# Two layers of a network, image by image: layer 0 of the next image worked off in pieces between the steps of layer 1

## The chip, the cores and the metric

The kernel runs on one core of a Trainium2 chip. A core has a matrix engine (PE, with its weight loads listed apart as PEld), a vector engine (DVE), a scalar engine (ACT), a general engine (POOL), queues that start transfers (SP's is the one used here for images), an on-chip memory SBUF of 128 partitions, and a small accumulator memory PSUM in eight banks that PE writes. Every engine takes its instructions in a fixed order, and instructions of different engines wait for each other through semaphores. The metric is the device time of one execution in microseconds; lower is better.

## The reference

The input x is [8, 256, 64, 64] in float32: 8 images, 256 channels, 64×64 pixels. Each layer normalises x in 32 channel groups (mean and variance per image and group) and adds its result to x. What matters of the code, cut:

```python
# layer 0 (x is the normalised input)
x1, x2, x3 = conv1x1(x, w1), conv1x1(x, w2), conv1x1(x, w3)      # 32, 32, 256 channels
h = relu(bn(concat([x1, unfold3x3(reflect_pad(x2))])))            # 320 channels
h = relu(bn(conv1x1(h, cw1)))                                     # 32 channels
w = conv1x1(h, cw2)                                               # 32 groups x 9 taps per pixel
out0 = sum over 9 taps of unfold3x3(zero_pad(x3)) * w             # 8 channels share a group's weights
x = x + out0
# layer 1 (x normalised again)
q, k, v = conv1x1(x, Wq) / 8, conv1x1(x, Wk), conv1x1(x, Wv)      # 4 heads of 64
att = softmax(q . (unfold7x7(k) + position))                      # 49 neighbours of a pixel
out_att = att @ unfold7x7(v)
wts = softmax over 9 of conv1x1(x, Wfc)                           # 9 weights per channel and pixel
oc = dwconv3x3(relu(dwconv3x3(x, w1)), w2)
out1 = rate1 * out_att + rate2 * sum over 9 of oc * wts
x = x + out1
```

## The kernel before

Channels lie on partitions, in two halves (ct = 0, 1); an image is cut into 8 bands of 8 rows, so that a tile [128, 512] is one half of one band. The images run strictly one after the other: all of layer 0, then all of layer 1, each with pools of its own. A band of x stays in SBUF from its load to its store (`xpool`, 10 band tiles): layer 0 writes its result over it, and layer 1 adds to it. The zero-padded map x3 (`x3p`) and the normalised padded image (`yp`, 70×70) are whole images and share one buffer. The order of instructions on each engine is made when the program is built, by a scheduler that follows program order and free buffers; a buffer with n copies lets n users be in flight.

Layer 0, with L numbers of the profile: `small_maps` (one matmul pair p12 and six ACT writes into x2s), `value_maps` (p3, L260, then an ACT write into x3p), `hidden_maps` (three relu writes, three matmuls ph at L283, h2), `products` (three pw matmuls at L295 into one tile of three banks, one DVE multiply of 128×1536 at L300, one POOL add of 128×1536 at L305), and `add_up` (an ACT copy of x into PSUM at L312, three DVE adds at L313 to L315, then bn_stats at L168 for the normalisation of layer 1). The loop staggers them by hand: maps of band i, hidden of band i − 1, products of band i − 2.

Layer 1 starts with `gn_affine` (normalisation constants), writes yp with ACT (L352) and the reflected pads with POOL. Then per band: `values` (pv matmuls at L418, ACT copies, transposes pvt at L432, ACT copies vt at L434), `place` (position term, POOL, L443), and for each ct `queries_keys` (pq L459, pk L475, DVE adds kb at L479, a POOL copy at L470), `depthwise` (ACT starts acc at L548 and L566, DVE taps at L560 and L573, ACT copy oc at L578) and four m-steps. An m-step is `probabilities` (mask and scores sco at L496 and L500, nmax on DVE at L505, exponentials and scaling on ACT at L510 and L515, the reciprocal tot on DVE at L513), the `weighted_values` of the step before (transposes ptp L522, ACT copy pt L524, 16 po matmuls L529) and `branch_weights` (two pf results of two matmuls each at L588, ACT exponentials ex at L593, and from the second step a DVE add of 128×1024 at L595). After the fourth step `dynamic_sum` closes the half: L603 adds the two halves of the sum on DVE, L604 bounds it, L606 takes the reciprocal `rec`, POOL multiplies twice (L608, L610), and DVE adds the result to x (L611); L390 adds po. Then the band is stored and band i of the next image is loaded into the freed tile, with its bn_stats.

PSUM in layer 0 is two `gen` banks and two pw tiles of three banks; in layer 1 three `gen` banks (pv, pvt, pq, pk, pf), two for sco, one each for po, acc and ptp.

## Time and profile before

| what | value |
|---|---|
| median of 3 runs (lowest to highest) | 5641.66 us (5640.54 to 5642.27) |
| profiled execution, its own time | 5641.8 us |
| its span (first to last instruction) | 5639.2 us |
| mean granted PE clock | 0.965 |
| busy: PE, DVE, ACT, POOL | 5083.2, 4177.2, 3052.5, 1392.0 us |
| DMA traffic | 76.36 MB, mean 14 GB/s |
| landing of one x load, one store | 3.7 us, 2.7 us |

The profile is one execution. Its groups give for each line of the kernel the busy time, the mean length of one instruction in ns, and what the engine waited for before it. The windows give the busy time of every engine in a stretch of the span. The chain of waits follows the work that ended last back to what released it. A busy PE is not PE at its peak, since the ends of matmuls are modelled.

### The profile page before, as it was taken

Reading aid. Unit: us, or ns where it says so; the run is one execution under the profiler, and the core shown is the slowest. Engines: PE = TensorE matmul, PEld = TensorE weight load, DVE = VectorE, ACT = ScalarE, POOL = GpSimd, SP = SyncE. Lnnn points to the kernel's source line nnn. Section 1 sums busy time; section 2 is a strip of 40 time slices with the busy share of each in tenths; the row PEclk is TensorE's granted clock in tenths of the full one; section 3 lists DMA queues with packets and bytes.
Section 4 is the critical chain, followed back from the end, with each engine's and each line's share of the span. In section 5 each row is a group of like instructions: output and inputs, shape, how many; then the busy total and the mean of one; then the engine's idle time right before and its main releaser. Section 6 shows DMA issues by size and latency. Waiting matters only on the chain.

```text
span 5639.2 us, 71792 instructions
## 1 busy us (share of the span) xinstructions
PE 5083.2 (90%) x28064; PEld 2489.7 (44%) x28064; DVE 4177.2 (74%) x5709; ACT 3052.5 (54%) x7026; POOL 1392.0 (25%) x889
## 2 busy tenths in 40 slices
PE   6799987999879998799987999879998799997998
PEld 2345433454334543354433544335543354433544
DVE  5688756887568875688766887668866688666886
ACT  3466644665436654466544665446664466544665
POOL 3411044111441114411144111531115311153111
PEclk9899998999989999899998999989999899998999
DMA  1000000000000000000000000000000000000000
GB/s 71 1 16 20 20 8 0 16 23 16 8 0 16 23 16 8 1 16 23 16 8 1 16 23 16 8 1 23 16 16 8 1 23 16 12 4 1 12 8 12
DMA packets 37922, 76.36 MB, mean 14 GB/s; under 512 B 2768, under 2 KB 4432, under 8 KB 37328
## 3 DMA queue, kind: packets, MB, share of 16 engines
q1 hardware_dynamic: 34816, 67.12, 3.6%
q8 instruction: 221, 3.62, 0.3%
q10 hardware_dynamic: 2768, 4.66, 0.2%
q14 instruction: 117, 0.96, 0.1%
HBM read 38.22 MB, written 33.55 MB: 13 GB/s over the span
## 4 chain that ended last, share of the span: by engine, by line
PE 46%; DVE 30%; ACT 11%; POOL 9%; issue 4%; DMA 1%; POOLq 0%; ACTq 0%; DVEq 0%; SPq 0%
PE pf L588 19%; PE pw L295 7%; DVE rec L606 7%; DVE acc L573 4%; PE po L529 4%; POOL prod L305 4%; DVE prod L300 4%; PE p L260 4%; PE ptp L522 3%; DVE acc L560 3%; PE ph L283 3%; POOL ex L608 3%; POOL oc L610 3%; ACT ex L593 2%; PE sco L500 2%
## 5 line engine op out<-in xcount | busy, mean ns | idle before, releaser
L588 PE MATMUL pf<-yp,c_wfc 128*128 128x512 f32 x4096 | 2026.8, 614 | 0.0
L305 POOL TENSOR_TENSOR prod<-prod,prod 128x1536 f32<-128x1536 f32 x256 | 880.8, 3441 | 536.1 <-DVE prod L300 530.5
L300 DVE TENSOR_TENSOR prod<-pw,x3p 128x1536 f32<-128x1536 f32 x384 | 665.3, 1752 | 387.0 <-PE pw L295 381.7
L588 PEld LDWEIGHTS pf<-yp,c_wfc 128*128 128x128 f32 x4096 | 692.5, 188 | 566.7 <-issue 528.8
L593 ACT ACTIVATE ex<-pf 128x512 f32<-128x512 f32 x1024 | 609.4, 597 | 581.4 <-PE pf L588 574.3
L560 DVE SCALAR_TENSOR_TENSOR acc<-yp,c_chan,acc 128x504 f32<-128x504 f32 (+3 forms) x1104 | 773.0, 700 | 184.7 <-ACT acc L548 165.9
L573 DVE SCALAR_TENSOR_TENSOR acc<-hid,c_chan,acc 128x504 f32<-128x504 f32 (+3 forms) x1024 | 755.1, 737 | 91.2 <-ACT acc L566 74.8
L295 PE MATMUL pw<-h,c_c 64*128 64x512 f32 x2304 | 711.7, 652 | 82.9 <-DVE prod L300 82.6
L595 DVE TENSOR_TENSOR ex<-ex,ex 128x1024 f32<-128x1024 f32 x384 | 469.8, 1223 | 245.6 <-ACT ex L593 243.7
L608 POOL TENSOR_TENSOR ex<-ex,rec 128x512 f32<-128x512 f32 x128 | 162.5, 1270 | 1971.4 <-DVE rec L606 1769.4
L510 ACT ACTIVATE prob<-sco,nmax 128x196 f32<-128x196 f32 x1024 | 425.3, 422 | 245.5 <-DVE nmax L505 243.9
L295 PEld LDWEIGHTS pw<-h,c_c 64*128 64x128 f32 x2304 | 278.3, 197 | 501.1 <-issue 315.1
L515 ACT ACTIVATE prob<-prob,tot 128x196 f32<-128x196 f32 x1024 | 412.7, 454 | 88.0 <-DVE tot L513 81.3
L529 PEld LDWEIGHTS po<-pt,vt 112*64 112x64 f32 (+1 forms) x8192 | 281.7, 137 | 366.8 <-ACT pt L524 330.8
L524 ACT COPY pt<-ptp 112x512 f32<-112x512 f32 x512 | 299.6, 585 | 243.4 <-PE ptp L522 241.5
L606 DVE RECIPROCAL rec<-ex 128x512 f32<-128x512 f32 x128 | 427.9, 3343 | 0.3
L522 PE MATMUL ptp<-ident,prob 128*112 128x128 f32 x2048 | 337.0, 284 | 46.0 <-ACT prob L515 46.0
L529 PE MATMUL po<-pt,vt 112*64 112x64 f32 (+1 forms) x8192 | 353.5, 228 | 15.6 <-ACT pt L524 11.8
L418 PE MATMUL pv<-yp,c_wv 128*128 128x280 f32 (+1 forms) x1152 | 314.8, 420 | 57.9 <-POOL yp L366 47.2
L443 POOL TENSOR_TENSOR pe<-pecol,perow 128x560 f32<-128x560 f32 (+1 forms) x64 | 77.7, 1214 | 1128.9 <-DVE kb L479 1110.0
L505 DVE TENSOR_REDUCE nmax<-sco 128x2 f32<-128x392 f32 x512 | 284.0, 555 | 67.4 <-PE sco L500 66.1
L522 PEld LDWEIGHTS ptp<-ident,prob 128*112 128x112 f32 x2048 | 211.1, 133 | 230.0 <-ACT prob L515 120.4
(118 smaller groups left out, 5785.8 us busy)
## 6 DMA issues: line engine op xcount, KB each, us to landing
x<-in_x SPq DMA_DIRECT2D x64, 512.0 KB, 3.7
out_x<-x SPq DMA_DIRECT2D x64, 512.0 KB, 2.7
c_wfc<-in_wfc ACTq DMA_DIRECT2D x1, 2304.0 KB, 14.9
c_c<-in_c ACTq DMA_DIRECT2D x1, 640.0 KB, 8.1
c_w<-in_w ACTq DMA_DIRECT2D x1, 256.0 KB, 6.9
c_wq<-in_wq ACTq DMA_DIRECT2D x1, 256.0 KB, 7.9
c_wk<-in_wk ACTq DMA_DIRECT2D x1, 256.0 KB, 8.6
c_wv<-in_wv ACTq DMA_DIRECT2D x1, 256.0 KB, 9.9
```

What stands on the lines that cost most here:

```text
L295: nc.tensor.matmul(pw[:, dj], c2[s, k // NG, ct * P : (ct + 1) * P], h2[s, :], start=True, stop=True)
L300: nc.vector.tensor_mul(prod.rearrange("p k (r c) -> p k r c", r=R), pw, bass.AP(v.tensor, v.offset, [v.ap[0], (1, 3), v.ap[1], v.ap[2]]),)
L305: nc.gpsimd.tensor_add(sums[0], sums[0], prod)
L510: nc.scalar.activation(prob[:, h, :NKEY], sco[:, h, :NKEY], AF.Exp, bias=nmax[:, h : h + 1], accum_out=tot[:, h : h + 1])
L522: nc.tensor.transpose(ptp[:, h, ch], prob[:, h, ch * CHUNK : (ch + 1) * CHUNK], ident)
L529: nc.tensor.matmul(po[h * HD : (h + 1) * HD, :, (2 * m + t) * TQ : (2 * m + t + 1) * TQ], vts[ch][m][:n, t, (2 * ct + h) * HD : (2 * ct + ...
L560: nc.vector.scalar_tensor_tensor(o, yp[:, ct, ra + dr : rb + dr, ca + dc : cb + dc], chan[:, ct, CW1 + k : CW1 + k + 1], o, ALU.mult, ALU.add,
L573: nc.vector.scalar_tensor_tensor(o, hid[:, ra + dr : rb + dr, ca + dc : cb + dc], chan[:, ct, CW2 + k : CW2 + k + 1], o, ALU.mult, ALU.add,)
L588: nc.tensor.matmul(pf, wfc[:, kt, 2 * m + j, ct * P : (ct + 1) * P], yp[:, kt, i * R + PAD : i * R + PAD + R, PAD : PAD + W], start=(kt == ...
L593: nc.scalar.activation(ex[:, j].rearrange("p (r c) -> p r c", r=R), pf, AF.Exp)
L595: nc.vector.tensor_add(ex, ex, tot)
L606: nc.vector.reciprocal(rec, tot)
```

## The change

Layer 0 becomes a generator of small pieces, each with a weight: begin 1, small_maps 4, value_maps 4 per half, hidden_maps 6, products 3 for each of six groups, and zero for statistics and store: 36 per band, 289 per image. Layer 1 becomes a generator that yields twice in each m-step, 128 times per image. All layer 0 of image 0 and the pieces of 24 further steps (LEAD) are issued first; then each yield adds 289/128 to a credit, and pieces of the next images are issued as long as the credit covers them. So the pieces of layer 0 of image b + 1 stand in program order between the m-steps of layer 1 of image b.

Both layers now share all pools. All layer-0 results in PSUM (p12, p3, ph, pw) use the three gen banks of layer 1. Images no longer stay in SBUF: x is loaded twice (for its statistics, `x_s`, and for the work, `x_c`), the layer-0 result of each band is stored to a DRAM tile `x1`, and layer 1 reads it twice: as `xr` (the residual) and as `yp`, now a band tile of 14 rows with three buffers, filled by up to six transfers, then normalised in place on ACT and padded on POOL. All three kinds of x tile share five buffers. x2, x3 and vc become band tiles, and halo rows are copied by POOL.

Some operations move or change size. The multiply of 128×1536 becomes three of 128×512, the POOL add too; `add_up` becomes one POOL add to x (called xb in the text). The ex add of 128×1024, the add of the two halves and the last add to x go from DVE to POOL. The oc copy on ACT takes the scale rate2. ex has three buffers where it had four. The core of the diff:

```diff
+LEAD = 24
-    xpool = ctx.enter_context(tc.tile_pool(name="xpool", bufs=10))
-    img = ctx.enter_context(tc.tile_pool(name="img", bufs=1))
+    w0 = ctx.enter_context(tc.tile_pool(name="l0", bufs=2))
+    w1 = ctx.enter_context(tc.tile_pool(name="l1", bufs=2))
+    ps = ctx.enter_context(tc.tile_pool(name="ps", bufs=1, space=PSUM))
+    dram = ctx.enter_context(tc.tile_pool(name="dram", bufs=3 * NB, space=DRAM))
+    def x_tile(name):
+        return w0.tile([P, NCT, BAND], F32, tag="x", name=name, bufs=5)
...
+        def products(i, ct, di):
+            for dj in range(3):
+                k = 3 * di + dj
+                s = slice(k % NG * KG, (k % NG + 1) * KG)
+                pw = ps.tile([P, R, W], F32, tag="gen", name=f"pw_{b}_{i}_{ct}_{k}", bufs=3)
+                nc.tensor.matmul(pw, c2[s, k // NG, ct * P : (ct + 1) * P], h2s[i][s, :], start=True, stop=True)
+                prod = w0.tile([P, R, W], F32, tag="prod", name=f"prod_{b}_{i}_{ct}_{k}", bufs=5)
+                nc.vector.tensor_mul(prod, pw, x3s[i][:, ct, di : di + R, dj : dj + W])
+                if k == 0:
+                    sums[ct] = prod
+                else:
+                    nc.gpsimd.tensor_add(sums[ct], sums[ct], prod)
+            if di == 2:
+                xb = xs[i][:, ct, :]
+                nc.gpsimd.tensor_add(xb, xb, sums[ct].rearrange("p r c -> p (r c)"))
+                bn_stats(im.st1, xs[i], ct, i)
+        def store(i):
+            t = dram.tile([P, NCT, BAND], F32, tag="x1", name=f"x1_{b}_{i}")
+            im.x1.append(t)
+            nc.sync.dma_start(out=t, in_=xs[i])
+        yield 1, begin
+        for i in range(NB + 1):
+            if i < NB:
+                yield 4, lambda i=i: small_maps(i)
+                yield 4, lambda i=i: value_maps(i, 0)
+                yield 4, lambda i=i: value_maps(i, 1)
+            if b + 1 < B and i:
+                yield 0, lambda i=i: first_stats(b + 1, i - 1)
+            if i:
+                yield 6, lambda i=i: hidden_maps(i - 1)
+                for ct in range(NCT):
+                    for di in range(3):
+                        yield 3, lambda i=i, ct=ct, di=di: products(i - 1, ct, di)
+                yield 0, lambda i=i: store(i - 1)
+    def padded_band(b, i):
...
+        yp = w1.tile([P, NCT, RP, WP], F32, tag="yp", name=f"yp_{b}_{i}", bufs=3)
...
+        for ct in range(NCT):
+            nc.sync.dma_start(out=yp[:, ct, PAD : PAD + R, PAD : PAD + W], in_=x1[i][:, ct])
+            if i:
+                nc.sync.dma_start(out=yp[:, ct, :PAD, PAD : PAD + W], in_=x1[i - 1][:, ct, R - PAD :])
+            if i < NB - 1:
+                nc.sync.dma_start(out=yp[:, ct, PAD + R :, PAD : PAD + W], in_=x1[i + 1][:, ct, :PAD])
...
-        nc.scalar.copy(oc, acc)
+        nc.scalar.activation(oc, acc, AF.Copy, scale=rate2)
...
-        ex = w1.tile([P, 2, BAND], F32, tag="ex", name=f"ex_{nm}_{m}", bufs=4)
+        ex = w1.tile([P, 2, BAND], F32, tag="ex", name=f"ex_{nm}_{m}", bufs=3)
...
-            nc.vector.tensor_add(ex, ex, tot)
+            nc.gpsimd.tensor_add(ex, ex, tot)
...
-        nc.vector.tensor_add(tot, tot, even)
+        nc.gpsimd.tensor_add(tot, tot, even)
...
-        nc.vector.scalar_tensor_tensor(xs[i][:, ct], o, rate2, xs[i][:, ct], ALU.mult, ALU.add)
+        nc.gpsimd.tensor_add(xr[:, ct], xr[:, ct], o)
...
+    work = [list(layer0(b)) for b in range(B)]
+    steps = NB * NCT * NT
+    total = sum(w for w, f in work[1])
+    def advance(passes):
+        nonlocal credit
+        credit += passes
+        while queue and queue[0][0] <= credit:
+            w, f = queue.pop(0)
+            credit -= w
+            f()
+    advance(sum(w for w, f in work[0]) + total * LEAD / steps)
     for b in range(B):
+        for _ in layer1(b):
+            advance(total / steps)
```

In layer 1 the yp band i + 2 is prepared in the third m-step of band i's first half, and bands 0 and 1 of the next image in the last band's second half. The names, shapes and operations of the rest are unchanged.

## The prediction

> **What bounds the kernel now.** I read the busy row and the slices first, then the windows of the stages, then the chain of waits, then the groups.

> ```profile
> PE 5083.2 (90%) x28064; PEld 2489.7 (44%) x28064; DVE 4177.2 (74%) x5709; ACT 3052.5 (54%) x7026; POOL 1392.0 (25%) x889
> PE   6799987999879998799987999879998799997998
> POOL 3411044111441114411144111531115311153111
> 41.00:232.00 191.00, 160.01 (x441) 61.61 (x440) 127.14 (x123) 70.23 (x113) 112.34 (x35) 0.93 0.00 0
> 232.00:260.00 28.00, 20.12 (x81) 14.63 (x82) 10.22 (x20) 23.59 (x39) 4.55 (x18) 0.78 0.00 1
> 730.00:742.00 12.00, 4.28 (x17) 4.06 (x18) 5.30 (x17) 0.20 (x1) 2.52 (x2) 0.50 0.27 88
> 1864.00:1923.00 59.00, 58.32 (x378) 29.87 (x377) 51.35 (x75) 36.51 (x92) 7.21 (x7) 1.00 0.06 19
> ```

> The four windows give length, then busy time of PE, its weight loads, DVE, ACT and POOL, then the granted clock. They are layer 0 of image 0 (191 us), the start of its layer 1 (28), the gap before image 1 (12) and one steady layer-1 band (59.0). An image takes about 700 us. In a steady layer-1 band PE is busy 58.32 of 59.00 at clock 1.00: PE is the limit. Outside the steady bands PE loses: about 31 us in layer 0, 8 and 8 at the two seams. POOL works in layer 0 and almost rests in layer 1 (7.21 of 59).

> ```profile
> PE 46%; DVE 30%; ACT 11%; POOL 9%; issue 4%; DMA 1%; POOLq 0%; ACTq 0%; DVEq 0%; SPq 0%
> L305 POOL TENSOR_TENSOR prod<-prod,prod 128x1536 f32<-128x1536 f32 x256 | 880.8, 3441 | 536.1 <-DVE prod L300 530.5
> L300 DVE TENSOR_TENSOR prod<-pw,x3p 128x1536 f32<-128x1536 f32 x384 | 665.3, 1752 | 387.0 <-PE pw L295 381.7
> L595 DVE TENSOR_TENSOR ex<-ex,ex 128x1024 f32<-128x1024 f32 x384 | 469.8, 1223 | 245.6 <-ACT ex L593 243.7
> L608 POOL TENSOR_TENSOR ex<-ex,rec 128x512 f32<-128x512 f32 x128 | 162.5, 1270 | 1971.4 <-DVE rec L606 1769.4
> L606 DVE RECIPROCAL rec<-ex 128x512 f32<-128x512 f32 x128 | 427.9, 3343 | 0.3
> L603 DVE TENSOR_TENSOR ex<-ex 128x512 f32<-128x512 f32 x128 | 87.7, 685 | 0.8
> L479 DVE SCALAR_TENSOR_TENSOR kb<-pk,c_chan,pe 128x280 f32<-128x280 f32 (+1 forms) x288 | 138.3, 488 | 13.3 <-PE pk L475 13.3
> ```

> The chain of waits is PE for less than half and DVE for 30%: the queues hand over to each other closely. The groups give the prices: an add of 512 is 0.685 us on DVE (L603) and 1.270 on POOL (L608); one of 1536 is 3.441 on POOL. The add of 1024 on POOL has no row; between 1.270 and 3.441 a line gives 2.36 against DVE's 1.223 (L595).

> **What the change offers: the PE floor.** The matmuls stay. A layer-1 band cannot go under about 57.5 us of PE, a layer-0 band costs PE 18.8 when full; pw's nine 512-column matmuls per half alternate in pairs, and a stranger between them breaks the pairing, which I put at 2.5 us a band (between 0 and 4.5, by the 0.43 us that one record of a lone pw adds). Together 78.8 us for a joint band, against 59.2 + 19.8 = 79.0 now. So the floor gains nothing in the bands; what it removes is the lost PE time at the seams, 68 us per image (700 − 8 × 78.8). At this floor the program would take 5,370 us, worked out under the first rival.

> **What it moves to POOL.** Per image DVE loses L595 (48 × 1.223 = 58.7), L603 (16 × 0.685 = 11.0), L611 (12.9) and L313–315 (33.3), and gains about 15 by splitting 1752 ns products into three of 0.69: 522 to 421 us. ACT stays near 382 (the 512-wide copies into accumulators go, a wider yp normalisation comes; the two normalisations per image may cost up to two table loads of 1.28 each). POOL goes from 174 to about 419: product adds 128 × 1.27 = 162, ex adds 48 × 2.36 = 113, totals 20, multiplies 41, two residual adds 40, place, pads and halo copies 43. That is 54 us per joint band, below PE's 78.8. No engine's sum is the bound; the question is the waits.

> **Steady joint band, walked in queue order.** Every engine takes its queue in order, so an operation that waits holds those behind it.

> Step 1, between the channel halves. The last ex exp (0.60) now leads to POOL add 2.36, POOL add 1.27, then DVE tensor_scalar 0.42 and rec 3.34. Before, the kb adds (L479) of the next half stood ahead of rec; in the changed order they stand behind it. Starting from pq, kb ends at 0.8 + 2.4 + 1.3 + 0.4 + 3.4 + 2 × 0.49 ≈ 9.4 us. PE has pq, two pk pieces, ptp, po to do until 5.8, and its next matmul needs the bank that kb frees at 9.0: a stall of 3.2 us. Before, this cost nothing.

> Step 2, in the second half. bn_stats(st1) on DVE waits for POOL's xb add, which stands behind rec's two multiplies and the product adds (POOL lags by 13 us at that point, 1.27 per add). Behind bn_stats in DVE's queue stand the products whose reads free the three gen banks, so PE's pw and pf wait: 1.8 and 3.7 us. A stall already taken in step 1 lets POOL catch up, so I take half, 2.75 (range 0 to 5.5).

> Step 3, at the end of the band. rec → POOL multiply, multiply, xr add (3 × 1.27) → ACT oc copy, because oc has two buffers. In bands 1 to 3 of an image oc stands ahead of the next band's vt copies, acc and qb in ACT's queue, and vt frees the banks of pvt; in bands 4 to 7 it stands behind vt. From the last pf to the next band's first pf I count 21.9 us for 12.2 of PE work, a stall of 9.7, or 6.7 in the later bands: mean 7.8.

> Band: 78.8 + 3.2 + 2.75 + 7.8 = 92.6 us. All steps at full size give 95.3; step 3 alone gives 86.6; none gives 78.8.

> **Layer 0 of image 0, alone.** It has nothing beside it. Eighteen POOL adds of 1.27 (22.9) bound a band, plus about 6 us from halo copies through hid, ph, h2 to the first pw, since the pieces of one band now stand in program order without the two-band stagger: 29 us against 19.8. Start 41 + prologue 10 + (8 + 1.5 bands of lead) × 29 = 326 us until image 0's layer 1 begins (232 before).

> **The tail.** Layer-0 work ends 24 steps early, so image 7 and the end of image 6 (9.5 bands) run alone at about 64 us: 59.2 + 2.3 (kb behind rec) + 2.8 (oc behind POOL); 60 to 68.

> **Transfers.** x is read twice, the layer-0 result goes out and comes back twice, on SP's queue in order: x1 store (waits for xb), x_s, x_c, xr, six yp loads per band with rows of 256 B. These are 3,584 packets a band. A 2 KB packet of the x queue takes 3.6% × 16 × 5639 / 34816 = 0.093 us; at that price 3584 / 16 × 0.093 = 21 us, asked for more than a band ahead: hidden by the band, and I take zero (below zero is excluded, since all of it is added traffic; above, the third rival). [...]

> POOL's add keeps its length beside a busy DVE here: L305 runs from 3417 to 3462 ns over all 256. [...]

> **Sum.** 326 + 54.5 joint bands × 92.6 (5,047) + 7 images × 16.5 (values of band 0, 8.5; layer-1 normalisation and first yp, 8: 115) + 9.5 × 64 (608) + 9 (end, and 2.6 outside the span) = 6,105 us. The profiled run of before was 5641.8 (span 5639.2), as good as the median, 5641.66. Break-even is a joint band of (5641 − 326 − 115 − 608 − 9) / 54.5 = 84.1 us.

> **Rivals.**
> 1. PE-bound, faster: POOL's lag never reaches PE, as banks and buffers cover it. Band 79.5, tail 60: 326 + 4,333 + 115 + 570 + 9 ≈ 5,355. For it: no engine's sum passes PE, and POOL has 25 us of slack a band. Against it: three gen banks serve all of both layers, and kb and oc follow POOL chains of 4 to 8 us. It decides when the stalls sum to under 5.3 us a band; then the seams' 68 us win.
> 2. Only the end of the band stalls (step 3): 86.6, so 326 + 4,720 + 115 + 608 + 9 = 5,778, a slight loss. It decides if step 1's bank is freed in time and DVE never waits for xb.
> 3. DRAM traffic: 256-B rows at over 4.4 times 0.093 us make yp the wait; a band then takes 100 or more, 6,510. For it: the SP queue is one and in order; against: DMA is 1% busy.

> **Chances.** Forecast (bands of 88 to 100) 0.50; rival 2 with its neighbourhood (82 to 88) 0.20, of which a quarter lies under break-even; rival 1 0.24; rival 3 0.06. Faster 0.24 + 0.04 = 0.28; within 0.2% (about what this measurement can tell from nothing) 0.02; slower 0.70. The forecast's own range is 5,850 to 6,500; eight in ten needs rival 2 and the edge of rival 1: 5,420 to 6,500.

> **What would show it.** In the changed profile: joint bands of 88 to 97 us with PE busy 80 to 88% and POOL near 55 us; PE's idle put down to kb, to products on DVE, and to vt; DVE idle put down to POOL's xb and ex; 29 us per band before image 0's layer 1; bands of 64 at the end. Wrong if joint bands are under 84 us with PE above 95%, or if yp loads end the waits.

## The result, and the profile after

The changed kernel takes 6407.3 us (median of 4 runs, 6405.0 to 6408.6) against 5641.3 (4 runs): 1.136 times as long, 95% interval 1.134 to 1.138. The forecast was 6,105 us, slower, with a range of 5,420 to 6,500. The profiled run is 6405.0 us, its span 6403.2.

The busy row, the slices, the granted clock and the chain of the changed kernel:

```profile
PE 5583.4 (87%) x28064; PEld 2642.8 (41%) x28064; DVE 3437.2 (54%) x5453; ACT 3067.9 (48%) x6910; POOL 3282.2 (51%) x3049
...
PE   6788888888898888988898888988888988899988
...
PEclk8788999999999999999999999999999999999999
...
POOL 4744454554554545545455455544455454553443
...
PE 54%; POOL 21%; DVE 14%; ACT 5%; issue 4%; DMA 1%; POOLq 0%; SPq 0%; ACTq 0%; DVEq 0%
```

The work moved as the forecast had it: POOL 1392 to 3282 us (410 an image, 419 forecast), DVE 4177 to 3437 (430 an image, 421 forecast). No engine is the bound, and yet the span grew. PE's number of matmuls is the same, but its busy time rose by 500 us. About 340 of them are a lower clock: with PE's busy time laid on the profile's clock records, half speed cost 94 us in the kernel before and 434 here. What makes up the other 160 was not measured apart; the forecast had put 2.5 us in each of the 64 bands, 160 in all, on broken pairs of pw.

Windows of the changed kernel: layer 0 of image 0, one joint band (band 1 of image 2), one band of the tail. The columns are those of the windows before.

```profile
42.00:320.00 278.00, 227.29 (x460) 88.83 (x459) 120.38 (x196) 65.14 (x105) 189.94 (x194) 0.79 0.20 59
2055.30:2154.10 98.80, 85.91 (x433) 40.17 (x432) 52.36 (x80) 47.07 (x108) 51.22 (x47) 0.91 0.13 38
5930.00:5995.00 65.00, 57.85 (x362) 28.68 (x362) 46.28 (x71) 38.52 (x95) 27.27 (x23) 0.97 0.12 31
```

In the joint band PE is busy 85.9 of 98.8 us at a granted clock of 0.91: 85.9 × 0.91 = 78.2 us of full-speed work, close to the forecast's 78.8. The rest is idle (12.9) and slow clock (7.7). The product is an estimate, since the granted clock is a mean over the stretch with its idle time; the clock records laid on the busy time alone give 79.1 and 6.8. The idle is put down to these releasers, in the waits of PE over two joint bands:

```profile
PE pvt L456 <- ACT vt L458: 7.0, 2, 4.0
PE pf L611 <- DVE prod L313: 5.7, 2, 2.8
PE pw L311 <- DVE kb L502: 5.1, 2, 2.5
PE pvt L456 <- ACT vc L447: 3.8, 2, 2.4
PE pv L442 <- ACT ex L616: 2.8, 2, 1.4
PE pv L442 <- ACT x L251: 1.4, 2, 0.7
```

Halved, they are 2.5 us at kb (step 1), 2.8 at the products (step 2) and 7.5 at the end of the band, where step 3 lies. Of these 7.5, only 3.5 are the wait for vt that step 3 named; the other rows are vc, ex and the writes of x2s (L251). What each idle does to the clock is seen in PE's timeline (start, length, operation, idle before and its releaser) and in windows of 4 us around the first of them:

```profile
2193.60 0.69 PE L552 MATMUL po<-pt,vt 112*64 112x64 f32 x16
2196.83 1.12 PE L311 MATMUL pw<-h,c_c 64*128 64x512 f32 x2 [2.54 <-DVE kb L502]
...
2211.05 1.13 PE L311 MATMUL pw<-h,c_c 64*128 64x512 f32 x4
2215.00 3.62 PE L611 MATMUL pf<-yp,c_wfc 128*128 128x512 f32 x4 [2.83 <-DVE prod L313]
```

```profile
2190.00:2194.00 4.00, 4.00 (x30) 2.34 (x30) 1.33 (x2) 1.26 (x2) 2.52 (x2) 1.00 0.00 0
2194.00:2198.00 4.00, 1.46 (x16) 0.56 (x16) 3.80 (x5) 0.00 (x0) 1.40 (x2) 0.98 0.00 0
2198.00:2202.00 4.00, 4.00 (x12) 1.42 (x13) 1.77 (x3) 0.53 (x1) 4.00 (x4) 0.50 0.02 4
2202.00:2206.00 4.00, 4.00 (x7) 1.48 (x6) 3.73 (x7) 2.98 (x9) 3.64 (x4) 0.67 0.00 0
2206.00:2210.00 4.00, 4.00 (x25) 1.63 (x24) 3.39 (x7) 1.11 (x2) 1.59 (x2) 1.00 0.00 0
```

After 2.54 us of idle the clock is 0.50 for about four microseconds and 0.67 in the mean over the next four. This stall of 2.5 us thus cost about 6: 2.0 us are lost in the first four and 1.3 in the next. The forecast had no term for this in its bands.

The groups that answer to those of before, and two that show the new waits (the third number is the idle time of the engine ahead of the group):

```profile
L317 POOL TENSOR_TENSOR prod<-prod,prod 128x512 f32<-128x512 f32 x1024 | 1298.3, 1268 | 606.5 <-DVE prod L313 544.7
L618 POOL TENSOR_TENSOR ex<-ex,ex 128x1024 f32<-128x1024 f32 x384 | 903.4, 2353 | 1259.6 <-ACT ex L616 1259.6
L627 DVE TENSOR_SCALAR ex<-ex 128x512 f32<-128x512 f32 x128 | 75.8, 592 | 660.3 <-POOL ex L626 649.4
L177 DVE BATCH_NORM_STATS2 st<-x_c 128x6 f32<-128x512 f32 x128 | 88.9, 694 | 472.3 <-POOL x_c L320 472.3
L601 ACT ACTIVATE oc<-acc,c_rowp 128x512 f32<-128x512 f32 x128 | 88.0, 687 | 533.7 <-POOL xr L634 525.6
```

The POOL add of 1024 takes 2.353 us; the interpolation said 2.36. The last three rows are the three places where a queue stands still for POOL: ahead of rec (L627), at bn_stats (L177) and at the oc copy (L601). The experiments ask which of them costs PE time.

### The profile page after: what moved, and what is told of

It is laid out like the page before. It is cut to its first block, busy times and chain, and to the rows that moved or that the text cites. A ratio compares the mean times of both kernels' runs of the same rounds, so it can differ in the third digit from the quotient of the medians.

```text
span 6403.2 us, 75865 instructions
## 1 busy us (share of the span) xinstructions
PE 5583.4 (87%) x28064; PEld 2642.8 (41%) x28064; DVE 3437.2 (54%) x5453; ACT 3067.9 (48%) x6910; POOL 3282.2 (51%) x3049
## 3 DMA queue, kind: packets, MB, share of 16 engines
q1 hardware_dynamic: 293376, 223.39, 12.5%
## 4 chain that ended last, share of the span: by engine, by line
PE 54%; POOL 21%; DVE 14%; ACT 5%; issue 4%; DMA 1%; POOLq 0%; SPq 0%; ACTq 0%; DVEq 0%
PE pf L611 26%; PE pw L311 8%; POOL prod L317 8%; DVE rec L629 6%; POOL ex L618 4%; PE po L552 3%; PE sco L523 3%; PE ph L298 3%; PE p L276 3%; PE ptp L545 3%; POOL x_c L320 2%; POOL ex L626 2%; DVE prod L313 2%; PE pq L482 2%; DVE acc L583 2%
## 5 line engine op out<-in xcount | busy, mean ns | idle before, releaser
L611 PE MATMUL pf<-yp,c_wfc 128*128 128x512 f32 x4096 | 2157.0, 659 | 142.6 <-DVE prod L313 123.3
L317 POOL TENSOR_TENSOR prod<-prod,prod 128x512 f32<-128x512 f32 x1024 | 1298.3, 1268 | 606.5 <-DVE prod L313 544.7
L618 POOL TENSOR_TENSOR ex<-ex,ex 128x1024 f32<-128x1024 f32 x384 | 903.4, 2353 | 1259.6 <-ACT ex L616 1259.6
L611 PEld LDWEIGHTS pf<-yp,c_wfc 128*128 128x128 f32 x4096 | 779.8, 206 | 1113.0 <-issue 773.3
L311 PE MATMUL pw<-h,c_c 64*128 64x512 f32 x2304 | 957.6, 688 | 149.0 <-DVE kb L502 88.8
L313 DVE TENSOR_TENSOR prod<-pw,x 128x512 f32<-128x512 f32 x1152 | 752.2, 683 | 338.9 <-PE pw L311 317.0
L627 DVE TENSOR_SCALAR ex<-ex 128x512 f32<-128x512 f32 x128 | 75.8, 592 | 660.3 <-POOL ex L626 649.4
L601 ACT ACTIVATE oc<-acc,c_rowp 128x512 f32<-128x512 f32 x128 | 88.0, 687 | 533.7 <-POOL xr L634 525.6
```

Source lines behind the costliest of these rows:

```text
L311: nc.tensor.matmul(pw, c2[s, k // NG, ct * P : (ct + 1) * P], h2s[i][s, :], start=True, stop=True)
L313: nc.vector.tensor_mul(prod, pw, x3s[i][:, ct, di : di + R, dj : dj + W])
L317: nc.gpsimd.tensor_add(sums[ct], sums[ct], prod)
L611: nc.tensor.matmul(pf, wfc[:, kt, 2 * m + j, ct * P : (ct + 1) * P], yp[:, kt, PAD : PAD + R, PAD : PAD + W], start=(kt == 0), stop=(kt == ...
L618: nc.gpsimd.tensor_add(ex, ex, tot)
```

## The experiments

Theory T: the joint band is about 79 us of matmul work, 13 of idle behind chains that end on POOL, and the slow clock after it. Rival M: the mixing costs, because three gen banks serve two layers, whoever adds. The first four kernels:

**The three adds back on DVE.**

```diff
-            nc.gpsimd.tensor_add(ex, ex, tot)
+            nc.vector.tensor_add(ex, ex, tot)
...
-        nc.gpsimd.tensor_add(tot, tot, even)
+        nc.vector.tensor_add(tot, tot, even)
...
-        nc.gpsimd.tensor_add(xr[:, ct], xr[:, ct], o)
+        nc.vector.tensor_add(xr[:, ct], xr[:, ct], o)
```

> Edit: the ex add, the add of the two halves and the add to xr go back from POOL to DVE; all else as changed. Theory T (the joint band of 98.5 us is 79 us of matmul work, about 13 us of PE idle behind chains that pass through POOL, and about 6.5 us of matmul time at the lowered clock that follows these idles): the chain ahead of rec gets 1.7 us shorter (2.36 to 1.22, 1.27 to 0.69), the one behind it 0.6; the stall at kb falls from 2.7 to about 1 us and takes no clock any more, the end of the band loses 2 to 3 us of idle: band about 92, time about 6050. Rival M (the mixing itself: two layers through three gen banks stall PE whoever does the adds): DVE's 10 us more per band delay the products that free the banks: no gain, 6400 or more.

Measured: 6047 us, 360 less. Three joint bands take 269.6 us for 297.8 (image 3, bands 1 to 3). The bands of image 7, which have no layer 0 beside them, fall to 58.7 to 60.1 us (64.5 in the first, and not counting the last, which runs to the end of the kernel), where they had been 64.2 to 68.2: with the adds on DVE, layer 1 alone is back at the 59.2 of before. T holds, and M has no account of it.

**bn_stats later in program order.**

```diff
-                bn_stats(im.st1, xs[i], ct, i)
+                late.append((xs[i], ct, i))        # issued ahead of the next half's third product group
...
```

> Edit: bn_stats of a layer-0 half is issued one half later, so that DVE does not wait for POOL's last add to x; the add itself stays where it is. T: the stall of pf behind a product behind bn_stats (3.4 us in a joint band) goes, and with it the half clock that follows: 5 us a band, time about 6130. Rival M: the bank wait comes back at the next product, since the banks are short anyway: under 1 us a band, 6350 or more.

Measured: 6407 us, no change. That is M's number and not T's, but the timelines of DVE show that the edit did not do what it was meant to; of the changed kernel:

```profile
2209.95 0.56 DVE L528 TENSOR_REDUCE nmax<-sco 128x2 f32<-128x392 f32 x1
2213.66 0.69 DVE L177 BATCH_NORM_STATS2 st<-x_c 128x6 f32<-128x512 f32 x1 [3.16 <-POOL x_c L320]
2214.28 0.67 DVE L313 TENSOR_TENSOR prod<-pw,x 128x512 f32<-128x512 f32 x1
```

and of this one:

```profile
2211.17 0.56 DVE L537 TENSOR_REDUCE nmax<-sco 128x2 f32<-128x392 f32 x1
2214.89 0.69 DVE L177 BATCH_NORM_STATS2 st<-x_c 128x6 f32<-128x512 f32 x1 [3.16 <-POOL x_c L322]
2215.50 0.67 DVE L315 TENSOR_TENSOR prod<-pw,x 128x512 f32<-128x512 f32 x1
```

The order on DVE is the same, although bn_stats stands later in the program. The likely reason, which no run shows, is that the scheduler takes bn_stats where it reckons its input ready. On the chip the input comes after 3.16 us of idle, and the product behind it waits too. The run says nothing about the cost of that wait.

**Three oc buffers.** `bufs=2` to `bufs=3` for oc.

> Edit: three oc buffers for two. T: oc on ACT no longer waits for the add to xr on POOL, so the vt copies behind it in ACT's queue come earlier in bands 1 to 3 of an image; the stall of pvt (4.3 us) shrinks to about 1: 4 to 6 us in three of eight bands, 1 to 2 in the others, time about 6270. Rival M: pvt waits for its bank anyway: 6390 or more.

Measured: 6376 us, 31 less, a quarter of what T expected. In image 3 the first joint band fell from 98.5 to 94.7 us, and bands 1 to 3 stayed at 99: a third buffer seems only to put the wait off by one copy while oc stands ahead of vt.

**No mixing.** All layer-0 pieces of an image ahead of layer 1 of the image before:

```diff
-    advance(sum(w for w, f in work[0]) + total * LEAD / steps)
+    advance(sum(w for w, f in work[0]) + 0.5)
     for b in range(B):
+        advance(total)
         for _ in layer1(b):
-            advance(total / steps)
+            pass
```

> Edit: the layer-0 pieces of an image are all issued ahead of layer 1 of the image before, nothing is mixed into layer 1; pools, pieces, DRAM bands and POOL adds as changed. T: nothing hides the pieces' own POOL chain: layer 0 about 33 us a band as measured for image 0 (264 an image), layer 1 about 66 as in the tail (528), 25 at the seams: 817 an image, about 6540. Rival M (the mixing is what costs): layer 0 near 22 us a band and layer 1 near 61: 690 to 720 an image, 5650 to 5800.

Measured: 6628 us; an image takes 822 (expected 817 by T): from the first query matmul of an image's last band to that of the next image it is 361 us, of which about 67 are that band, so that layer 0 and the seam take 294; the seven other bands average 66. Before, these were 223 (282 less 59) and 59. So the mixing itself gains: 822 to 789 us an image. What loses is the rest of the change: the pieces in their new form (+71 us an image, the three shared banks among them) and layer 1 in its new form (about +6.5 us in each of 8 bands, which the bands of image 7 in the first run put on the adds). That mixing is what costs, as M has it, is out.

The next four set orders by force, with an edge that puts one instruction behind another on the same engine (`behind(later, earlier)`), without any semaphore.

**kb ahead of rec.** `behind(<bounded sum of half 0>, <last kb add of half 1>)`

> Edit: an order edge on DVE puts the kb adds of the second half ahead of the bounded sum and rec of the first; nothing else. T: the stall of PE at kb (2.5 us of idle in a joint band, and the low clock after it) goes; as the products behind rec still free the banks of pw and pf late, part of it comes back there: 2 to 4 us a band, about 6240 (6180 to 6330). Rival M: the bank wait takes its place in full, 6390 or more.

Measured: 6390 us, 17 less. M's number, but not for all of M's reason: over the run PE's wait at kb before pw (88.8 us) is gone, and its wait for products ahead of pf rises from 123.3 to 264.7 us, that of pvt for vt from 101.7 to 137.3:

```profile
PE pf L624 <- DVE prod L319: 264.7, 90, 3.9
```

By the program's order, the products that free the banks stand behind the same rec. Step 1 was a real wait with a successor in line.

**bn_stats one band later, by force.** `behind(bn_stats(...), <sixth of the nine products of the later half>)`

> Edit: bn_stats of a layer-0 half is put one band later by an order edge behind a product of that later half, so that the scheduler cannot pull it forward again; its POOL add is then long done. T: the stall of pf (2.8 to 3.4 us a joint band) goes with the low clock behind it: about 6180 (6100 to 6280). Rival P (POOL's lag stands behind it all: with five product buffers the next product waits for the same adds): the wait moves from bn_stats to a product and PE stalls as before: 6380 or more.

Measured: 6001 us, 406 less, more than any theory had. The bn_stats row of this kernel:

```profile
L183 DVE BATCH_NORM_STATS2 st<-x_c 128x6 f32<-128x512 f32 x128 | 87.6, 684 | 29.9 <-POOL x_c L328 29.9
```

Idle ahead of it falls from 472.3 to 29.9 us. Three joint bands take 268.1 us, at a clock of 0.96 for 0.91. Rival P is wrong: products then wait 46.9 us for POOL over the whole run, no more. The surplus over T has a reason in PE's waits. That of pf for products falls from 123.3 to 9.4 us, but most of what PE waited for at the end of the band goes too, the wait of pvt for vt above all, first in the changed kernel and then here:

```profile
PE pvt L456 <- ACT vt L458: 101.7, 38, 4.5
PE pvt L471 <- ACT vt L473: 17.0, 38, 1.1
```

The oc copy still waits 453.1 us for POOL in this run (525.6 before the edge). So the end of the band hung on bn_stats as well as on oc.

**oc behind vt.** `behind(<oc copy>, <last vt copy>)`

> Edit: an order edge on ACT puts the oc copy of a band's first half behind the vt copies of that band. T: in bands 1 to 3 of an image the stall of pvt (4.3 us and about 3 of low clock) goes, so that they take the 92 to 94 us of bands 4 and 5: 5 us in three of eight bands, 6290 (6250 to 6330). Rival M: pvt then waits for its bank: 6390 or more.

Measured: 6101 us, 306 less; 6290 was expected. ACT's idle ahead of oc falls from 533.7 to 16.0 us:

```profile
L608 ACT ACTIVATE oc<-acc,c_rowp 128x512 f32<-128x512 f32 x128 | 89.6, 700 | 16.0 <-DVE tot L543 7.5 <-DVE acc L603 6.7 <-POOL ex L625 0.9
```

PE's wait of pvt for vt falls from 101.7 to 3.2 us, and that of pf for products from 123.3 to 80.3. Bands 1 to 3 fall by 9 to 10 us each, not 5, and bands 4 and 5, which had the right order already, still by 6 and 1.

**The adds and the orders together, with three oc buffers.**

> Edit: the three adds back on DVE, the three order edges, three oc buffers. T: the joint band falls from 89.5 with the adds alone to 83 or 84 as the stalls at products and vt go: about 5720 (5620 to 5850). Rival M: 6000 or more.

Measured: 5780 us, within T's range; bands 1 to 3 take 255.6 us, 85.2 each where T had 83 or 84, at a clock of 0.97.

**The orders alone**, adds on POOL and two oc buffers, is the control for that:

> Edit: the three order edges alone; the adds stay on POOL. T: the order of the queues is the larger part of the loss: the stalls at bn_stats (406 us alone) and at oc (306 us alone) overlap in part: about 5850 (5780 to 5950). Rival A (the adds on POOL are too slow in themselves): 5950 or more, since POOL's chain ahead of rec stays.

Measured: 5851 us, on T's number to a microsecond, which is luck: T's sum for the overlap was a guess between 5780 and 5950. So the three edges, with the places in the program that they need, remove no instruction and give 556 of the 766 us that the change lost. Moving the adds to DVE and adding the third oc buffer then gives only 71 more (5851 to 5780), where the adds alone gave 360 without the edges: a slow engine is dear where another queue stands behind it.

**Another order of the pieces**, value_maps between the product groups, alone:

> Edit: the other order of the pieces alone, adds on POOL, no order edges. T: bn_stats still waits for POOL's last add, but the products come earlier in the band: 2 to 4 us a band and 40 to 60 us at the start: about 6200 (6080 to 6350). Rival: the scheduler packs the queues as before: 6350 or more.

Measured: 6406 us; the rival is right. The image period falls by 5 us (789 to 784), and the first image's start is 30 us later. With the waits for POOL in place, a smoother program order buys nothing. With everything else in place it does:

> Edit: as the run with adds and orders, and the layer-0 pieces in another order: small_maps(i), hidden_maps(i-1), then the six product groups of band i-1 with the two value_maps(i) behind the first and second of them. T: products no longer come in a burst in the second half, the halo-to-product bubble of image 0's own layer 0 is partly covered: joint band 82 to 84, bands 6 and 7 of an image about 95, start 40 to 60 us earlier: about 5560 (5480 to 5680), that is faster than before. Rival M: no change from 5780.

Measured: 5649 us (ratio to before 1.0012, interval 1.0003 to 1.0022), better than the 5780 by 131 and within the expected range, but above 5560 and not faster than before. The joint bands came down as expected (247.8 us for bands 1 to 3 of image 3, 243 to 252 in images 0 to 5), but the first query matmul came at 398 us, not 40 to 60 earlier than 358: in the layer 0 of image 0, with nothing beside it, hid waits for halo copies that stand behind product adds in POOL's queue (in one case 3.5 us behind eight adds in a row), and PE waits 27 us for hid in these 250. Hence the last kernel, with an order of its own for image 0:

```diff
+        halo = nc.vector if b == 0 else nc.gpsimd
...
+                    eng = nc.vector if b == 0 and ct == 1 and k < 5 else nc.gpsimd
+                    eng.tensor_add(sums[ct], sums[ct], prod)
...
+        if b == 0:
+            for i in range(NB + 2):
+                for n in range(2 * 3):
+                    if i > 1:
+                        yield 3, lambda i=i, ct=n // 3, di=n % 3: products(i - 2, ct, di)
+                    if n == 0 and i < NB:
+                        yield 4, lambda i=i: small_maps(i)
+                    if n in (1, 2) and i < NB:
+                        yield 4, lambda i=i, mt=n - 1: value_maps(i, mt)
+                    if n == 3 and 0 < i <= NB:
+                        yield 6, lambda i=i: hidden_maps(i - 1)
...
```

> Edit: as the run with adds, orders and spread pieces, but image 0, whose layer 0 has nothing beside it, gets a staggered order of its own (products of band i-2 between the maps of band i), its halo copies on DVE and the first four adds of each second half on DVE. T: the start (first query matmul at 398 us in the run before, 255 before the change) comes down to about 310, the rest stays: about 5565 (5530 to 5610), that is 1.0 to 1.9% faster than before. Rival: image 0's start is held by the loads and the normalisation and not by the order: 5620 or more.

Measured: 5570.9 us against 5641.8, ratio 0.988 (0.986 to 0.990): 1.2% shorter than the kernel before, 13% shorter than the changed one. The first query matmul comes at 333 us. Its page:

```profile
PE 5221.2 (94%) x28064; PEld 2513.0 (45%) x28064; DVE 4012.1 (72%) x6155; ACT 3059.6 (55%) x6910; POOL 2043.0 (37%) x2347
...
PE   6889998999989999899998999999998999999998
...
PEclk9899999999999999999999999999999999999999
```

Three joint bands of this kernel, and the same three of the changed one below it:

```profile
2475.20:2718.70 243.50, 234.22 (x1293) 111.62 (x1291) 182.53 (x271) 140.43 (x319) 97.00 (x114) 1.00 0.16 44
```

```profile
2842.40:3140.20 297.80, 259.04 (x1293) 120.37 (x1292) 157.01 (x240) 140.79 (x319) 153.76 (x142) 0.91 0.13 36
```

The matmuls are as many (1293). Busy time by clock gives 234.2 × 1.00 = 78.1 us a band here and 259.0 × 0.91 = 78.6 there. In the runs between (adds 251.0 × 0.96, bn_stats 249.7 × 0.96, oc 247.5 × 0.96, orders 243.5 × 0.96, both 241.3 × 0.97) the same product is 78 to 80 a band. The full-speed work is constant within this estimate; idle and clock are what changes. At 81.2 us a band the kernel is about 3 us from the floor in these three bands (243 to 248 us in images 0 to 5). It is further off in the first band of an image (84 us) and in bands 6 and 7 (103 and 91 to 93), where PE is busy 88 us each and, in image 4, waits longest for kb (4.4 us over both) and for the normalisation's small DVE steps (d_a, 3.1 and 2.0). What would shorten these was not tried.

## Why the prediction was right, and where it was off

The direction, the mechanism and the range held. By its own steps, the bands being bands 1 to 3 of an image:

| term | forecast | measured |
|---|---|---|
| full-speed PE work of a joint band | 78.8 us | 78.6 (259.0 × 0.91 / 3) |
| idle: kb, products, end of band | 3.2, 2.75, 9.7 (7.8 as the mean of all bands) | 2.5, 2.8, 7.5 |
| slow clock in a joint band | no term | 7.7 (86.3 − 78.6); 7.4 over the busy time alone |
| image period (8 bands and seam) | 757 (8 × 92.6 + 16.5) | 789 |
| first query matmul of image 0 | 343 (326 + 16.5) | 378 |
| image 7 from there to the end | 521 | 541 |

**The mis-sized term** is the band. Bands 1 to 3 were forecast at 94.5 us (78.8 + 3.2 + 2.75 + 9.7) and took 99; over an image the forecast's mean was 92.6, and the measured period less its 16.5 for the seam gives 96.5. The idle in bands 1 to 3 was smaller than forecast, 12.9 for 15.7; what the forecast lacked is the slow clock. Over the 788.1 us of image 1's period the trace gives 642 of work at full speed, 94 of idle and 52 of slow clock, where the forecast held 630, 110 and 16.5 for the seam. The forecast had read the granted clock of 0.50 to 0.78 in the gaps of the kernel before and of 1.00 in its steady bands, and did not ask what gaps inside a band would do. Between the first query matmuls of image 0 and image 7 the kernel took 5,484 us, where the forecast's terms give 5,242 (54.5 × 92.6, six seams of 16.5, 1.5 bands of 64): 242 of the 302 us that it was short. The start adds 35 and the tail 20.

**What each step was worth** was off too, though the idle of each was near its forecast. Step 1 looked like a cost of 3.2 us a band; taking it away gave 17 us in all, since the products took over its wait. That this wait for products doubled with step 1 gone (123.3 to 264.7 us) agrees with the forecast's halving of step 2. Step 2 had been put at 2.75 us a band; removing it gave 6.6 us an average band of an image (788.9 to 736.2 us over eight), with the clock behind the idle and with most of the wait for vt, which the forecast had put on oc alone. Step 3's idle came near its size, but less than half of it was the wait for vt; removing the oc wait gave 37.5 us an image, 4.7 a band. The effects overlap: 17 + 406 + 306 = 729 alone, 556 together.

**Rival 1** (PE-bound, about 5,355) did not occur in the changed kernel. Its condition, stalls under 5.3 us a band, agrees with the last kernel, which has 3.1 of idle a band in bands 1 to 3 and is faster than before. That kernel is 216 us above the rival's figure, nearly all of it in the joint images: their period is 685 us against 652.5 (8 × 79.5 + 16.5), with bands 6 and 7 far above 79.5. **Rival 2** (only the end of the band) did not occur. **Rival 3** (transfers): no transfer stands among the long waits of PE. The queue of the image transfers used 12.5% of 16 engines for 293,376 packets, 0.044 us a packet, less than half of the 0.093 that the forecast had taken from the 2 KB packets. By size, a 256-byte row took 0.021 us in the mean and a 2 KB packet 0.104: the small rows are 1.6 times as dear by the byte, but too cheap by the piece to matter here.

Some of the prediction's sums are slightly off, and its total does not hang on them: 419 us of POOL an image are 52 a joint band and not 54 (measured 51.2), 700 − 8 × 78.8 is 70 and not 68, the announced 5,370 is 5,353 by the first rival's terms, and a quarter of 0.20 is 0.05.

## What to carry to other kernels

When work is moved to a slower engine, its busy sum says little. Ask which instruction of another queue waits for the moved one, and what stands behind it: here two such places, a statistics instruction and a copy, and the order of kb and rec cost 556 us together, and the fix was three order edges. Moving an instruction in the program need not move it in its engine's queue, as the second experiment showed; look in the timeline for an instruction that waits at the head of a queue, and hold it back with an explicit edge. Remove such waits one at a time and together, since each alone may hide or feed another. And price a PE stall with the slow clock that can follow it: in the changed kernel it added half again or more (6.8 to 7.7 us on 12.9).

## What the runs showed of the hardware

**Twenty short DVE instructions ended just behind a POOL add.** The bounded sum, a tensor_scalar of 512, took 412 to 428 ns in the kernel before; in the changed one the median is 427 but the longest 1474, and the mean 592. Twenty of the 128 took 1469 to 1474 ns, and each of them had started 71 to 77 ns after a POOL product add and ended about 0.28 us behind it; the POOL add of 512 takes 1268. What held them is not shown. In the whole run it is 22 us on DVE. It did not happen behind every POOL instruction: 41 others overlapped short POOL copies (229 to 239 ns) and kept their 426 to 429 ns. The POOL product adds themselves keep their length (1257 to 1332 ns).
